# Second biases of a graph layer and a mixture of experts: from a product in the output sums to rows loaded under the experts' results

## The chip, the cores and the metric

The kernel runs on one core of one Trainium2 chip. The core has five engines that each work through their own instructions in order: TensorE (PE: matrix products and transposes, with its weight loads shown apart as PEld), VectorE (DVE), ScalarE (ACT), GpSimd (POOL) and SyncE (SP). They wait for each other by semaphores. SP, ACT and POOL also issue transfers (DMAs), which 16 DMA engines carry out. The metric is the time of one execution on the device in microseconds (us); lower is better.

## The reference, cut to what matters

625 rows of 1024 numbers pass through a graph convolution over 20,000 edges and then through a mixture of experts. The change concerns the second part alone, for x normalised:

```python
sh = _gelu(jnp.einsum('td,sdh->sth', xf, sW1) + sb1[:, None, :])
shared = jnp.einsum('sth,shd->std', sh, sW2) + sb2[:, None, :]
shared = shared.mean(axis=0)
gates = xf @ rW + rb
topk_vals, topk_idx = jax.lax.top_k(gates, TOP_K)
topk_probs = jax.nn.softmax(topk_vals, axis=-1)
...
h = _gelu(jnp.einsum('td,edh->eth', xf, W1) + b1[:, None, :])
y = jnp.einsum('eth,ehd->etd', h, W2) + b2[:, None, :]
moe = jnp.einsum('te,etd->td', w, y)
return (shared + moe).reshape(B, L, D)
```

There are two shared experts and eight others, of which each row uses two (TOP_K), with weights that sum to one. The second biases are sb2 (2 x 1024) and b2 (8 x 1024).

## The kernel before

The kernel computes only what each row needs. One program holds the whole: a sparse path, and a dense one that runs only when the sparse path's tables overflow. The recording layer orders the instructions of each engine; `tc.issue_after` pins some of them, and the names below are those of the profile.

*The start.* SP loads the edges, x (xh), the graph weights (wg). POOL makes constants and issues small loads: rb_t (five), vec (two), bd (two), rw_t. Then VectorE makes one-hot matrices of the edges (ohs at L873 and L874, ohk at L877) and statistics of the rows (st at L776), and TensorE counts edges with them (cnt) and projects the rows (p_pr, L920). After the graph layer, normalised rows (h2) and sums (x1d) are written to DRAM.

*Routing.* `gate`, `route` and `slots` choose two experts per row and give each choice a place (slot) in one of NJ = 11 tiles of 128 rows. Seven tiles belong to one expert each (4 to 10), three (0 to 2) to two with 64 rows each, one (3) to four with 32 rows each. `ej` holds the expert numbers, read into registers (`e_of`), and `row` the row of the table `yt` in DRAM to which each slot's result goes. `wab` holds the two weights of each row.

*Experts.* For each tile POOL gathers its rows (`fetch`, into io tiles, three buffers), TensorE transposes and multiplies them (`expert_in`, p_h; `expert_mid`, p_hT). Then, in the order ORDER = 4, 5, 6, 0, 1, 2, 3, 7, 8, 9, 10, it multiplies by the second weights (p_yj, L1455; two halves of 512 columns, each in one of five banks of the tag acc). The halves are copied out (L1459 on VectorE, L1461 on ACT) to a tile ys, which POOL scatters to rows of yt (L1463). ys tiles, the copies w2m of second weights and the rows g read back from yt share the 15 buffers of the pool gat.

*Output.* SP loads the shared experts' second weights (sw2, L1434) and the sums x1 (five tiles of 125 rows, L1437) when the buffers of the first weights come free, and after the last scatter the rows g (L1474). TensorE makes the shared experts' sums p_o (eight products per block, L1510), VectorE adds half of it and the two weighted rows g to x1 (L1486), and SP and ACT store the rows.

*The biases.* `bias_parts` brings sb2 and b2 from the DRAM tile bd into the bfloat16 tile b23, split into three parts for accuracy; `weights_T` does the same with the rows' weights (1 for the shared ones, twice the softmax weight for the others) and has TensorE transpose them (p_wT, L1336) into wT. One more product per block, wT by b23 (L1512), puts all biases into p_o:

```python
            with tc.issue_after(made.ins):
                for i in range(NS):
                    for k in range(HK):
                        nc.tensor.matmul(p[:TP, :n], shT[:, i, k, own], sw2[:, i, k, at],
                                         start=(i == 0 and k == 0), stop=False)
                nc.tensor.matmul(p[:TP, :n], wT[:, own], b23[:, at], start=False, stop=True)
            add(x1[:, d, at], p[:TP, :n], 1.0 / NS, x1[:, d, at])
```

Of the kernel before, what the change touches and what calls it, by code (L numbers as in the profile page):

```python
# [18 lines left out]
N = 625  # L19
# [434 lines left out]
def sparse_kernel(  # L454
# [171 lines left out]
    for i in (2, 3):  # L626
        nc.gpsimd.tensor_add(join, join, ident[:, QC * i : QC * (i + 1)])


    bd = dram.tile([3, NS + NE, D], F32, name="bd")  # L630
    nc.gpsimd.dma_start(bd[:, :NS, :], bass.AP(tensor=sb2.tensor, offset=sb2.offset,
                                               ap=[[0, 3], [D, NS], [1, D]]))
    nc.gpsimd.dma_start(bd[:, NS:, :], bass.AP(tensor=b2.tensor, offset=b2.offset,
                                               ap=[[0, 3], [D, NE], [1, D]]))
    b23 = const.tile([3 * QC, D], BF16, name="b23")

    def bias_parts():
        b2x = io.tile([3 * QC, D], F32, tag="io", name="b2x")
        nc.vector.memset(b2x, 0.0)
        for j in range(3):  # L640
            nc.gpsimd.dma_start(b2x[j * QC : j * QC + 3 * (NS + NE)], bd.rearrange("i e d -> (i e) d"))
        b2h = rt.tile([3 * QC, D], BF16, name="b2h")
        for j in range(3):
            with tc.issue_after(named.ins):
                nc.vector.tensor_copy(b2h, b2x)
            nc.scalar.copy(b23[j * QC : (j + 1) * QC], b2h[j * QC : (j + 1) * QC])
            if j < 2:
                nc.vector.tensor_sub(b2x, b2x, b2h)

    rw_t = const.tile([128, KD, QC], F32, name="rw_t")  # L650
    nc.vector.memset(rw_t[:, :, NE:], 0.0)
# [369 lines left out]
    def clear():  # L1021
        nc.gpsimd.memset(zero, 0.0)
        for a in range(2):
            to = bass.AP(tensor=yt.tensor, offset=yt.offset + (a * YB + 1) * D,
                         ap=[[NT * D, 128], [D // 2, 2 * NT], [1, D // 2]])
            nc.sync.dma_start(to, zero[:, None, :].to_broadcast([128, 2 * NT, D // 2]))

    at(50, clear)
    at(100, last_rows)
    at(30, transpose_vec)  # L1030
# [101 lines left out]
        nc.vector.tensor_copy(gates, pv[:, :, :NE])  # L1132


    w = const.tile([TP, NT, NS + NE], F32, name="w")
    wT = hid.tile([3 * QC, N], BF16, name="wT")
    sel = const.tile([TP, NT, NE], F16, name="sel")
    wide = [TP, NT, NE]

    def route():  # L1140
        full = [TP, NT, NE, NE]
        other = gates[:, :, None, :].to_broadcast(full)
        own = gates[:, :, :, None].to_broadcast(full)
        nc.vector.tensor_scalar(lower, lower, 0.0, None, op0=ALU.is_gt)
        above = rt.tile(full, F32, name="above")
        equal = rt.tile(full, F32, name="equal")
        nc.vector.tensor_tensor(above, other, own, op=ALU.is_gt)
        nc.vector.tensor_tensor(equal, other, own, op=ALU.is_equal)
# [15 lines left out]
        nc.vector.memset(w[:, :, :NS], 1.0)  # L1164
        nc.vector.tensor_mul(w[:, :, NS:], ex, inv[:, :, None].to_broadcast(wide))


    shT = hid.tile([128, NS, HK, N], F32, name="shT")
# [19 lines left out]
    def slots():  # L1188
# [66 lines left out]
        nc.vector.tensor_mul(m, m, w[:, None, :, NS:].to_broadcast(both_))  # L1255
# [61 lines left out]
        nc.vector.tensor_tensor(flag, flagf[:, 0:1], flagf[:, 1:2], op=ALU.add)  # L1317
        return named

    def weights_T():  # L1320
        nc.vector.tensor_scalar(w[:, :, NS:], w[:, :, NS:], float(NS), None, op0=ALU.mult)
        NW_ = NS + NE
        part = rt.tile([TP, NT, 3 * QC], F32, name="part")
        nc.vector.memset(part, 0.0)
        near = const.tile([TP, NT, NW_], BF16, name="near")
        for i in range(3):
            nc.vector.tensor_copy(near, w)
            for j in range(3):
                at = j * QC + i * NW_
                nc.vector.tensor_copy(part[:, :, at : at + NW_], near)  # L1330
            if i < 2:
                nc.vector.tensor_sub(w, w, near)
        for a, b in ((0, 3), (3, NT)):
            p = ps_mm(f"p_wT_{a}")
            for d in range(a, b):
                nc.tensor.transpose(p[: 3 * QC, (d - a) * TP : (d - a + 1) * TP], part[:, d, :],  # L1336
                                    ident[:TP, :TP])
            nc.vector.tensor_copy(wT[:, a * TP : b * TP], p[: 3 * QC, : (b - a) * TP])

    gate()  # L1340
    route()
    named = slots()
    weights_T()
    bias_parts()
    for t in range(HK):
        shared_in(1, t)
    sh_in.close()
# [4 lines left out]
    xts = ExitStack()  # L1352
    xt = pool(xts, "xt", 2, side="right")
    _, e_of = nc.values_load_multi_w_load_instructions(
        ej, engines=[mybir.EngineType.PE, mybir.EngineType.Activation], min_val=0, max_val=NE - 1,
        skip_runtime_bounds_check_because="a count of eight ends at most, cut to seven")


# [69 lines left out]
    xts.close()  # L1428
    in_w.close()

    late = pool(ctx, "late", side="right")
    sw2 = late.tile([128, NS, HK, D], F32, name="sw2")
    for i in range(NS):
        nc.sync.dma_start(sw2[:, i], sW2[i].rearrange("(k p) d -> p k d", p=128))  # L1434
    x1 = late.tile([TP, NT, D], F32, name="x1")
    for t in range(NT):
        nc.sync.dma_start(x1[:, t, :], x1d[t * TP : (t + 1) * TP, :])  # L1437
    gat = pool(ctx, "gat", 15, side="right")

    ORDER = (*whole[:3], *range(NM2), *whole[3:])  # L1440
    w2m = {}
    for j in ORDER:
        for a, _, e in parts(j)[1:]:
            for k in range(HK):
                w2m[j, a, k] = gat.tile([128, D], F32, tag="y", name=f"w2m_{j}_{a}_{k}")
                nc.scalar.copy(w2m[j, a, k][:, None, :], w2a[:, bass.ds(e, 1), k, :])
    sent = []
    for n, j in enumerate(ORDER):
        y = gat.tile([128, D], F32, tag="y", name=f"ys_{j}")
        for s in range(2):  # L1450
            at = slice(s * 512, (s + 1) * 512)
            p = ps_acc(f"p_yj_{j}_{s}")
            for k in range(HK):
                for a, b, e in parts(j):
                    made = nc.tensor.matmul(p[a:b], hjT[:, j, k, a:b],  # L1455
                                     w2m[j, a, k][:, at] if a else w2a[:, bass.ds(e, 1), k, at],
                                     start=(k == 0), stop=(k == HK - 1))
# [12 lines left out]
    for d in range(NT):  # L1470
# [26 lines left out]
    for d in range(NT):  # L1497
        if d == LATE:
            for i in range(d, NT):
                add_experts(i)  # L1500
        own = slice(d * TP, (d + 1) * TP)
        for at in ((0, 512), (512, D)) if d < NT - 1 else ((0, 512), (512, 768), (768, D)):
            n = at[1] - at[0]
            at = slice(*at)
            p = (ps_mm if banks % 8 > 4 else ps_acc)(f"p_o_{d}_{at.start}")
            banks += 1
            with tc.issue_after(made.ins):
                for i in range(NS):
                    for k in range(HK):
                        nc.tensor.matmul(p[:TP, :n], shT[:, i, k, own], sw2[:, i, k, at],  # L1510
                                         start=(i == 0 and k == 0), stop=False)
                nc.tensor.matmul(p[:TP, :n], wT[:, own], b23[:, at], start=False, stop=True)  # L1512
# [48 lines left out]
```

## Time and profile before

| | us |
|---|---|
| median of 3 runs | 295.12 |
| lowest and highest | 292.23, 295.93 |
| the profiled execution | 294.8 |
| its span, first to last instruction | 293.0 |
| PE busy | 283.4 (97%) |
| DVE busy | 168.3 (57%) |
| ACT busy | 103.2 (35%) |
| POOL busy | 44.1 (15%) |

The profile is of one execution, so durations and positions are compared with its own 294.8 us. Busy time is that of an engine's instructions; a wait counts to none. A chain of waits is followed back from the last instruction: at each step to what released it, or to the instruction before it on its engine. "Granted clock" is TensorE's clock as a share of full speed; DMA share is the mean busy share of the 16 DMA engines.

### The profile page before, as it was taken

To read this page: it belongs to the slowest core of one execution; us is meant where nothing else is said; L and a number is where in the kernel's file an instruction comes from. 1 tells how busy PE (TensorE), PEld (TensorE's weight loads), DVE (VectorE), ACT (ScalarE), POOL (GpSimd) and SP (SyncE) were. 2 spreads that over 40 slices of the span, in tenths; PEclk is the share of its full clock that TensorE was granted. 3 is DMA by queue.
4 is the path that set the end of the run, shared out by engine and by line. 5 is a ranking of instruction groups with operands and counts; after the bars stand their busy time and mean duration, and the time that the engine had idled before them with its cause. 6 is when DMAs were issued, how large, how long until landed. Compare 5 with 4: busy or idle time off the path is not lost.

```text
span 293.0 us, 4532 instructions
## 1 busy us (share of the span) xinstructions
PE 283.4 (97%) x1573; PEld 192.1 (66%) x1573; DVE 168.3 (57%) x459; ACT 103.2 (35%) x237; POOL 44.1 (15%) x101
## 2 busy tenths in 40 slices
PE   7998999999999999899999999999999999999992
PEld 5876777778888555677777987778643334444451
DVE  5699999997874888746925322222134111157920
ACT  2348425513642323353105544656198111000000
POOL 9500000000000024420131312110012223200000
PEclk9999999999999999999999999999999999999998
DMA  6999930000000999999999742420095545389351
GB/s 229 344 322 408 408 117 2 2 1 2 0 0 4 327 364 392 393 392 369 409 353 408 283 143 78 140 74 0 2 342 230 211 194 226 136 332 403 134 156 53
DMA packets 28699, 61.41 MB, mean 210 GB/s; under 512 B 2150, under 2 KB 15981, under 8 KB 28666
## 3 DMA queue, kind: packets, MB, share of 16 engines
q1 hardware_dynamic: 23144, 44.17, 42.0%
q0 software_dynamic: 5232, 16.55, 15.4%
q10 hardware_dynamic: 296, 0.35, 0.5%
q8 instruction: 15, 0.25, 0.3%
q14 instruction: 12, 0.10, 0.1%
HBM read 43.02 MB, written 18.81 MB: 211 GB/s over the span
## 4 chain that ended last, share of the span: by engine, by line
PE 77%; DVE 20%; issue 1%; ACT 1%; ACTq 0%; DVEq 0%
PE p_h L1397 13%; PE p_yj L1455 13%; PE p_o L1510 12%; PE p_sh L1175 11%; PE p_pr L920 9%; PE p_agg L937 5%; PE p_x L1378 3%; DVE ohs L873 3%; DVE ohs L874 2%; PE p_y L983 2%; PE scrap L1000 2%; DVE xh L987 2%; DVE st L776 2%; DVE xh L807 1%; DVE ohk L877 1%; DVE h L747 1%
## 5 line engine op out<-in xcount | busy, mean ns | idle before, releaser
L920 PE MATMUL p_pr<-wg,nT 128*125 128x286 f32 x240 | 61.5, 409 | 1.0 <-ACT nT L825 0.8
L920 PEld LDWEIGHTS p_pr<-wg,nT 128*125 128x125 f32 x240 | 43.8, 187 | 13.2 <-ACT nT L825 1.8
L1397 PE MATMUL p_h<-w1a,xsT 128*128 (+2 forms) x176 | 40.0, 381 | 0.0
L1455 PE MATMUL p_yj<-w2a,hjT 128*128 (+2 forms) x88 | 38.6, 595 | 0.0
L1510 PE MATMUL p_o<-sw,shT 128*125 128x512 f32 (+1 forms) x88 | 36.1, 554 | 0.0
L1175 PE MATMUL p_sh<-h2T,sw 128*128 128x313 f32 (+1 forms) x128 | 35.2, 429 | 0.0
L1397 PEld LDWEIGHTS p_h<-w1a,xsT 128*128 128x128 f32 (+2 forms) x176 | 28.8, 169 | 7.4 <-issue 0.5
L1175 PEld LDWEIGHTS p_sh<-h2T,sw 128*128 128x128 f32 x128 | 23.7, 190 | 8.6 <-issue 0.2
L1455 PEld LDWEIGHTS p_yj<-w2a,hjT 128*128 128x128 f32 (+2 forms) x88 | 14.4, 169 | 22.4 <-issue 22.4
L1510 PEld LDWEIGHTS p_o<-sw,shT 128*125 128x125 f32 x88 | 16.4, 188 | 16.9 <-issue 16.2
L1459 DVE COPY ys<-p_yj 128x512 f32<-128x512 f32 x15 | 10.4, 692 | 28.7 <-PE p_yj L1455 27.0
L1401 DVE COPY hj<-p_h 128x256 f32<-128x256 f32 x11 | 4.7, 425 | 31.1 <-PE p_h L1397 31.1
L994 POOL DMA_DIRECT2D x1d<-xh x10 | 5.3, 531 | 92.4 <-DVE flagf L721 89.0
L983 PE MATMUL p_y<-wo_t,eT 128*125 128x512 f32 (+1 forms) x40 | 18.8, 592 | 0.0
L1463 POOL DMA_INDIRECT yt<-ys,row x11 | 10.8, 981 | 50.5 <-DVE ys L1459 50.5
L1412 ACT ACTIVATE hjT<-p_hT,vT 128x128 f32<-128x128 f32 (+2 forms) x34 | 8.7, 332 | 24.5 <-PE p_hT L1409 24.5
L1486 DVE SCALAR_TENSOR_TENSOR x<-p_o,x 125x512 f32<-125x512 f32 (+1 forms) x11 | 6.9, 639 | 16.3 <-PE p_o L1512 16.3
L1370 POOL DMA_INDIRECT xs<-h2d,tok x11 | 10.4, 948 | 34.5 <-PE p_x L1378 24.9
L937 PE MATMUL p_agg<-P,CT 125*125 125x288 f32 x100 | 15.5, 305 | 0.0
L1397 PE MATMUL p_h<-w1m,xsT 128*64 128x256 f32 (+1 forms) x96 | 14.7, 382 | 0.0
L1455 PE MATMUL p_yj<-w2m,hjT 128*64 128x512 f32 (+1 forms) x48 | 14.1, 595 | 0.0
L1382 DVE COPY xsT<-p_x 128x512 f32<-128x512 f32 x11 | 7.6, 692 | 11.0 <-PE p_x L1378 8.7
(309 smaller groups left out, 422.8 us busy)
## 6 DMA issues: line engine op xcount, KB each, us to landing
w1a<-in_L_ffn_W_dram SPq DMA_DIRECT2D x8, 1024.0 KB
w2a<-in_L_ffn_W_dram SPq DMA_DIRECT2D x8, 1024.0 KB
yt<-zero SPq DMA_DIRECT2D x2, 2560.0 KB
g<-yt SPq DMA_DIRECT2D x10, 512.0 KB
sw<-in_L_ffn_sW_dram SPq DMA_DIRECT2D x4, 1024.0 KB
x<-x1d SPq DMA_DIRECT2D x5, 500.0 KB
x1d<-xh POOLq DMA_DIRECT2D x5, 448.0 KB, 7.2
h2d<-h POOLq DMA_DIRECT2D x5, 448.0 KB, 6.8
```

The source lines that it names most:

```text
L873: nc.vector.tensor_tensor(os, row[:, None].to_broadcast(shape), key, op=ALU.is_equal)
L920: nc.tensor.matmul(p[:TP, :F], nT[:, k, m * TP : (m + 1) * TP], wg[:, k, r, :], start=(k == 0), stop=(k == KD - 1))
L937: nc.tensor.matmul(p[:TP, : F + 2], CT[:, m, at : at + TP], P[:, m, r, i], start=(m == 0 and i == 0), stop=(m == NT - 1 and i == 1))
L983: nc.tensor.matmul(ps[s][:TP, :], eT[:n, k, :], wo_t[:n, k, at], start=(k == 0), stop=False)
L1175: nc.tensor.matmul(p[:, : z - a], sw1[:, i, k, t * 128 : (t + 1) * 128], h2T[:, k, a:z], start=(k == 0), stop=(k == KD - 1))
L1370: nc.gpsimd.indirect_dma_start(out=xs, out_offset=None, in_=h2d, in_offset=bass.IndirectOffsetOnAxis(ap=tok[:, j : j + 1], axis=0))
L1378: nc.tensor.transpose(p[:, k * 128 : (k + 1) * 128], xs[:, at : at + 128], ident)
L1397: nc.tensor.matmul(p[a:b, :H], xsT[j][:, k, a:b], w1m[j, a][:, 0, k, :] if a else w1a[:, bass.ds(e, 1), k, :], start=(k == 0), stop=(k == ...
L1455: made = nc.tensor.matmul(p[a:b], hjT[:, j, k, a:b], w2m[j, a, k][:, at] if a else w2a[:, bass.ds(e, 1), k, at], start=(k == 0), stop=(k = ...
L1459: nc.vector.tensor_copy(y[:, at], p)
L1463: sent.append(nc.gpsimd.indirect_dma_start(out=yt, out_offset=bass.IndirectOffsetOnAxis(ap=row[:, j : j + 1], axis=0), in_=y, in_offset=No ...
L1510: nc.tensor.matmul(p[:TP, :n], shT[:, i, k, own], sw2[:, i, k, at], start=(i == 0 and k == 0), stop=False)
```

## The change

The biases leave the output sums. At the start the kernel loads sb2 and b2 into a tile bt; `bias_table` makes b2 plus the mean of sb2 of it, one row for each of the eight experts, and writes it to bd in DRAM. As the two weights of a row sum to one, a row of that table under each of its two results gives the same sum. SP loads the table's row of each tile's expert, chosen by a register, into all of its ys tile's partitions (one transfer for a tile of one expert, two or four for the others) before the products are there, and VectorE adds each half product to it. The first three tiles of ORDER use io buffers, the others gat; the last five are asked for as the loop goes on. `weights_T`, `bias_parts`, wT, b23 and the product L1512 go.

```diff
-    bd = dram.tile([3, NS + NE, D], F32, name="bd")
...
+    BF = D * NE // 128
+    bd = dram.tile([NE, D], F32, name="bd")
+    bt = fbig.tile([128, NS + 1, BF], F32, name="bt")
+    for i in range(NS):
+        nc.gpsimd.dma_start(bt[:, i, :], bass.AP(tensor=sb2.tensor, offset=sb2.offset + i * D,
+                                                 ap=[[0, NE], [BF, D // BF], [1, BF]]))
+    nc.gpsimd.dma_start(bt[:, NS, :], b2.rearrange("e (q f) -> (e q) f", f=BF))
+
+    def bias_table():
+        nc.vector.tensor_add(bt[:, 0, :], bt[:, 0, :], bt[:, 1, :])
+        nc.vector.scalar_tensor_tensor(bt[:, NS, :], bt[:, 0, :], 1.0 / NS, bt[:, NS, :],
+                                       op0=ALU.mult, op1=ALU.add)
+        nc.gpsimd.dma_start(bd.rearrange("e (q f) -> (e q) f", f=BF), bt[:, NS, :])
...
+    at(46, bias_table)
     at(50, clear)
...
-    weights_T()
-    bias_parts()
...
-        ej, engines=[mybir.EngineType.PE, mybir.EngineType.Activation], min_val=0, max_val=NE - 1,
+        ej, engines=[mybir.EngineType.PE, mybir.EngineType.Activation, mybir.EngineType.SP], min_val=0, max_val=NE - 1,
...
+    ORDER = (*whole[:3], *range(NM2), *whole[3:])
+    ys, put = {}, {}
+
+    def bias_rows(j, y):
+        for a, b, e in parts(j):
+            put[j] = nc.sync.dma_start(y[a:b, :], bd[bass.ds(e, 1), :].to_broadcast([b - a, D]))
+        ys[j] = y
+
+    for j in ORDER[:3]:
+        bias_rows(j, io.tile([128, D], F32, tag="io", name=f"ys_{j}"))
...
+    for j in ORDER[3:6]:
+        bias_rows(j, gat.tile([128, D], F32, tag="y", name=f"ys_{j}"))
+    sw2 = late.tile([128, NS, HK, D], F32, name="sw2")
+    for i in range(NS):
+        with tc.issue_after(put[ORDER[5]].ins):
+            nc.sync.dma_start(sw2[:, i], sW2[i].rearrange("(k p) d -> p k d", p=128))
+    x1 = late.tile([TP, NT, D], F32, name="x1")
+    for t in range(NT):
+        with tc.issue_after(put[ORDER[5]].ins):
+            nc.sync.dma_start(x1[:, t, :], x1d[t * TP : (t + 1) * TP, :])
     sent = []
     for n, j in enumerate(ORDER):
-        y = gat.tile([128, D], F32, tag="y", name=f"ys_{j}")
+        y = ys[j]
...
-            if s or n < 4:
-                nc.vector.tensor_copy(y[:, at], p)
-            else:
-                nc.scalar.copy(y[:, at], p)
+            nc.vector.tensor_add(y[:, at], y[:, at], p)
...
+        if n + 6 < NJ:
+            bias_rows(ORDER[n + 6], gat.tile([128, D], F32, tag="y", name=f"ys_{ORDER[n + 6]}"))
...
-                nc.tensor.matmul(p[:TP, :n], wT[:, own], b23[:, at], start=False, stop=True)
```

More of the change, by code (lines that the diff above doesn't have):

```diff
@@ L627, in sparse_kernel @@
         nc.gpsimd.tensor_add(join, join, ident[:, QC * i : QC * (i + 1)])
-    bd = dram.tile([3, NS + NE, D], F32, name="bd")
[L631 to L648, printed above, removed]
+    BF = D * NE // 128
[10 more added lines that the diff above has]
+        nc.gpsimd.dma_start(bd.rearrange("e (q f) -> (e q) f", f=BF), bt[:, NS, :])
     rw_t = const.tile([128, KD, QC], F32, name="rw_t")
@@ L1132, in gate @@
         nc.vector.tensor_copy(gates, pv[:, :, :NE])
-    w = const.tile([TP, NT, NS + NE], F32, name="w")
-    wT = hid.tile([3 * QC, N], BF16, name="wT")
+    w = const.tile([TP, NT, NE], F32, name="w")
     sel = const.tile([TP, NT, NE], F16, name="sel")
@@ L1163, in route @@
         nc.vector.reciprocal(inv, tot)
-        nc.vector.memset(w[:, :, :NS], 1.0)
-        nc.vector.tensor_mul(w[:, :, NS:], ex, inv[:, :, None].to_broadcast(wide))
+        nc.vector.tensor_mul(w, ex, inv[:, :, None].to_broadcast(wide))
     shT = hid.tile([128, NS, HK, N], F32, name="shT")
@@ L1254, in slots @@
         nc.vector.tensor_tensor(m, m, ab[:, :, :, None].to_broadcast(both_), op=ALU.is_equal)
-        nc.vector.tensor_mul(m, m, w[:, None, :, NS:].to_broadcast(both_))
+        nc.vector.tensor_mul(m, m, w[:, None, :, :].to_broadcast(both_))
         nc.vector.tensor_reduce(wab, m, axis=AX.X, op=ALU.add)
@@ L1318, in slots @@
         return named
[L1320 to L1338, printed above, removed]
     gate()
@@ L1429, in sparse_kernel @@
     in_w.close()
-    late = pool(ctx, "late", side="right")
[L1432 to L1437, printed above, removed]
+    ORDER = (*whole[:3], *range(NM2), *whole[3:])
[6 more added lines that the diff above has]
+        bias_rows(j, io.tile([128, D], F32, tag="io", name=f"ys_{j}"))
+    late = pool(ctx, "late", side="right")
     gat = pool(ctx, "gat", 15, side="right")
-    ORDER = (*whole[:3], *range(NM2), *whole[3:])
     w2m = {}
@@ L1510, in sparse_kernel @@
                         nc.tensor.matmul(p[:TP, :n], shT[:, i, k, own], sw2[:, i, k, at],
-                                         start=(i == 0 and k == 0), stop=False)
-                nc.tensor.matmul(p[:TP, :n], wT[:, own], b23[:, at], start=False, stop=True)
+                                         start=(i == 0 and k == 0), stop=(i == NS - 1 and k == HK - 1))
             add(x1[:, d, at], p[:TP, :n], 1.0 / NS, x1[:, d, at])
```

## The prediction

> **What bounds the kernel now.** I read the page first: TensorE is busy 97% of the span. Then busy time by stage, cut where the chain of waits changes character (columns: stretch and length, then busy us of PE, PEld, DVE, ACT, POOL, granted TensorE clock, DMA share, GB/s):
>
> ```profile
> 11.80:52.00 40.20, 39.00 (x261) 30.24 (x259) 39.97 (x119) 19.22 (x54) 0.96 (x10) 1.00 0.71 249
> 123.90:213.20 89.30, 89.30 (x621) 69.21 (x622) 33.53 (x134) 37.50 (x78) 14.01 (x18) 1.00 0.62 221
> 213.20:250.60 37.40, 37.40 (x136) 14.53 (x135) 9.69 (x14) 17.08 (x27) 9.82 (x10) 1.00 0.60 239
> 250.60:287.20 36.60, 36.56 (x99) 17.59 (x98) 19.55 (x22) 0.00 (x0) 0.98 (x1) 1.00 0.63 232
> 287.20:293.00 5.80, 0.00 (x0) 0.00 (x0) 0.42 (x1) 0.00 (x0) 0.00 (x0) 0.87 0.11 31
> ```
>
> From 123.9 us on TensorE never stops: there, only TensorE's own work and new waits of TensorE count. From 11.8 to 52 us VectorE is full as well (39.97 of 40.20), and TensorE nearly so (39.00): a hole made there in either is not made up.
>
> The chain of waits, early, in the middle and late (start, us, what):
>
> ```profile
> 12.45 0.34 DVE ohs L873
> 12.80 0.02 issue
> 12.82 0.42 DVE ohs L874
> ```
>
> ```profile
> 147.45 0.54 PE p_wT L1336 x5
> ```
>
> ```profile
> 213.20 37.40 PE p_yj L1455 x134
> 250.60 3.43 PE p_o L1510 x8
> 254.03 0.22 PE p_o L1512
> ```
>
> The first shows the set end on VectorE's instructions back to back; the others what the bias path takes of TensorE.
>
> Then the queues that the change uses. POOL's early loads in the timeline, and the DMA issues of that stretch with KB each and us from issue to landing:
>
> ```profile
> 7.60 0.85 POOL L631 DMA_DIRECT2D bd<-in_L_ffn_sb_dram  x1
> 9.88 0.55 POOL L633 DMA_DIRECT2D bd<-in_L_ffn_b_dram  x1 [1.15 <-DMA rb_t<-in_L_ffn_rb_dram]
> ```
>
> ```profile
> bd<-in_L_ffn_b_dram POOLq DMA_DIRECT2D x1, 96.0 KB, 7.1
> rw_t<-in_L_ffn_rW_dram POOLq DMA_DIRECT2D x1, 32.0 KB, 7.4
> vec<-in_L_ffn_sb_dram POOLq DMA_DIRECT2D x1, 2.0 KB, 5.5
> ```
>
> SP's late issues in the timeline, and what SP's queue (q1) and POOL's (q0) moved from 211 to 219, from 219 to 248 and from 248 to 255 us (packets, MB, share of 16 engines):
>
> ```profile
> 211.81 1.50 SPq L1434 DMA_DIRECT2D sw<-in_L_ffn_sW_dram  x2
> 213.36 11.38 SPq L1437 DMA_DIRECT2D x<-x1d  x5
> ```
>
> ```profile
> q1 hardware_dynamic: 540, 2.09, 69.9%
> ```
>
> ```profile
> q0 software_dynamic: 1201, 3.87, 33.5%
> q1 hardware_dynamic: 646, 2.55, 22.2%
> ```
>
> ```profile
> q1 hardware_dynamic: 8, 0.02, 0.7%
> ```
>
> The 2.09 MB are the two sw2 loads (2 x 1024 KB), done by 219. The 2.55 MB are the five x1 loads (5 x 500 KB): 29 us at 0.088 MB/us, on 22.2% of 16, or 3.6 engines. They are slow and end at about 248, and nobody minds: VectorE's first add into x1 is at 254.3.
>
> **The change part by part.** The sum is made against the profiled execution, 294.8 us (span 293.0 and 1.8 around it); the median of the three runs, 295.12, is 0.3 above, inside their spread of 3.7.
>
> Removed from TensorE where it never stops: nine L1512 products of 0.22 us and the last two of 0.11 and 0.13, together 2.22; the five p_wT transposes, 0.54. **-2.76 us.** Leaving weights_T and bias_parts also frees VectorE (five 1024-wide passes alone are 3 x 0.69 + 2 x 1.22 = 4.5 us), ACT (3 x 1.04) and POOL (1.49 of b2x loads, so the first gathers leave earlier): nothing, since TensorE had 89.30 us of work in 89.30 throughout.
>
> Evictions: 22 adds on VectorE instead of 15 copies there and 7 on ACT. The nearest row, the add of a product to SBUF data of the same shape (L987), took 0.68 us, the copy 0.69. 22 x 0.68 = 15.0 us in a stretch of 37.4 on an engine with nothing else there: nothing, hidden by TensorE. If the adds have to wait, this cover goes; see below.
>
> The table, early. In the instruction order of the changed program bias_table does not stand at count 46: its first add is VectorE's instruction right behind the first one-hot comparison (ends 12.78), before L874 of the chain above. It waits for both sb2 loads. The first goes out where L631 did (7.60), the second where L633 did, at 9.88, as it waits for the same rb_t landing. Landing of POOL's small loads around it: 4.9 (rb_t, median), 5.2 and 5.5 (vec), 5.7, 7.1, 7.4 us. The load (32 KB in 128 pieces) falls between the last two in time; I take 6.3, between the vec rows and those two: 9.88 + 6.3 = 16.2, a stall of 3.4, and 0.2 for two 64-wide instructions. Behind it wait the one-hots, the second tile's statistics and thus transposes and projection: TensorE, out of its first projection at 15.5, waits as well, and neither has room to catch up. **+3.6 us**, bounds 2.1 (4.8 us) to 4.7 (7.4). The b2 load follows at 10.7 and lands at 17.0; VectorE needs it 2 us after the stall, at 18: nothing. The write of the table stands in POOL's queue before stores first due at 101.9, after 89 us of idleness: nothing.
> [...]
>
> The table, late. SP now reads the expert numbers too, behind the flag that it read at 145 us: nothing. Its queue becomes: ORDER[0..2] (tiles 4, 5, 6; io buffers, free by 204.5, landed well before 214), then six pieces for ORDER[3..5] from 211.8, then sw2, then x1, and only then ORDER[6..10]: tile 3 in four pieces, 7, 8, 9, 10. The three tiles ahead are 1.5 MB; at the 0.37 MB/us that sw2 had (213.3 to 219) they move sw2's end from 219 to 223.1. It is due at 250.4: nothing. But x1's start moves too. From 223.1 to about 242 (last scatter before the hold-up lands) at 0.088 MB/us or a little better, 1.7 MB; the rest, 0.85 MB, with no scatter beside it, at 0.124 (0.088 over 3.55 engines is 0.0248 an engine; 3.55 busy, with the scatters' 33.5% taken off each, are 3.55 / 0.665 = five engines in use): x1 ends at about 249. Tile 3's rows are queued behind it on those engines: 249 + 1.3 (32 KB an engine) + 1.2 until the landing is signalled (bounds 0 and 3.2, the shortest whole landing of a POOL transfer) = 251.5.
> Who waits: the add of ORDER[6], whose product TensorE has at 235.0. Behind it on VectorE wait all later adds; behind those the scatters, and TensorE once five acc banks are full. Halves run 1.72 us: five before the end of p_yj, TensorE needs that bank back, at 250.6 - 5 x 1.72 = 242.0. So it stands from 242.0 to 251.5 + 0.8 = 252.3: **+10.3 us.** Bounds: x1 at 0.124 throughout (ends 243.7) 3.8; at 0.088 throughout (252.1) and 3.2 until signalled 15.4. The remaining rows then follow one each 1.3 us or so, faster than TensorE asks. The tail (last scatter, reads of yt, adds) moves with it.
>
> After the stand TensorE's clock. In the last 5.8 us without a product the granted clock averages 0.87: how deep it falls no row tells. I assume one half: then it fell 4.3 us after the last product, and if it takes as long to return, 4.3 us at half speed lose **2.1 us**. Bounds 0 and twice that, 4.3; the middle, since no restart is in this trace.
> [...]
>
> Sum: 294.8 - 2.76 + 3.6 + 10.3 + 2.1 = **308.0 us**. Lowest: 294.8 - 2.76 + 2.1 + 3.8 = 297.9; highest: 294.8 - 2.76 + 4.7 + 15.4 + 4.3 = 316.4.
>
> **The rivals.**
> Not slower: tile 3's rows land by 241.2, because transfers behind x1 pass it. For it: x1 uses few engines, the others are free. Against: every piece spreads over partitions on all of them, so its last part waits. Then 294.8 - 2.76 + 3.6 = 295.6. It decides at 241.2, the 242.0 less 0.8.
> Faster or equal: besides that the early load lands before 12.8, in 2.9 us. The shortest landing of any POOL transfer was 3.2 (a scatter). 292.0 or, with the two instructions, 292.2.
> Slower still: 128 reads of one 4 KB row are slow. No row reads one row so often. At x1's 0.088 MB/us a tile of 0.5 MB takes 6 us; the last five, from 249 on, end at 279, and TensorE ends p_yj some 30 us late: 325. It decides above about 3.4 us a tile, TensorE's own pace.
>
> **How the numbers follow.** Hold-up behind x1: 0.80. No hold-up, early stall only: 0.10. All hidden: 0.04. Slow reads: 0.06. About 2% (5.9 us) is what a measurement of this kernel can tell from no change: below 289.2 faster, above 301.0 slower. Slower: 0.76 of the first (its low corner is under 301.0) and 0.06, 0.82; faster 0.01; the rest, 0.17, within. The range is the bounds of the first case, 298 to 316; the other three, 0.20, lie outside.
>
> **What would show it.** The changed profile should have L1512's and L1336's rows gone; VectorE idle for 3 to 4 us near 13 us "<-DMA bt"; one idle stretch of TensorE of some 10 us in p_yj, before the half that reuses the bank of ORDER[6]; VectorE's add of that tile waiting for "ys<-bd", SP's queue at 20 to 30% until then; a granted clock under 1.00 behind it. No idle TensorE there means x1 does not hold the rows. Adds that wait tile after tile mean slow reads.

## The result, and the profile after

The changed kernel takes 317.89 us (median of 4 runs, 317.35 to 318.51) where the kernel before takes 294.68 beside it (292.23 to 295.93): 1.080 times as long, 95% interval 1.072 to 1.088. The profiled execution took 318.29 us, its span 316.4, so 23.4 us more span than before. 308.0 was predicted, with 316 as the upper end: the direction and both places were right, the size was not.

Line numbers move: L1512 and L1336 are gone, p_yj is L1440, its adds L1443, row loads L1407, sw2 L1427, x1 L1431, p_o L1494, the table's first add L639.

VectorE's timeline of the changed kernel around the table (start, us, what, and in brackets the idle time before it and what ended it):

```profile
12.24 0.42 DVE L867 TENSOR_TENSOR ohs<-iota,cols 125x512 f16<-125x512 f16 x1
16.52 0.23 DVE L639 TENSOR_TENSOR bt<-bt 128x64 f32<-128x64 f32 x1 [3.86 <-DMA bt<-in_L_ffn_sb_dram]
16.66 0.42 DVE L868 TENSOR_TENSOR ohs<-ohs,cols 125x512 f16<-125x512 f16 x1
```

The second one-hot instruction stood at 12.82 before and stands at 16.66 now: 3.84 us. TensorE behind it, before and after, in each kernel's timeline of that engine:

```profile
15.76 1.07 PE L819 MATMUL p_t<-ident,h 125*128 125x125 f32 x8
16.87 4.12 PE L920 MATMUL p_pr<-wg,nT 128*125 128x286 f32 x16
```

```profile
19.60 1.93 PE L813 MATMUL p_t<-ident,h 125*128 125x125 f32 x8 [2.00 <-ACT h L780]
21.32 5.80 PE L914 MATMUL p_pr<-wg,nT 128*125 128x286 f32 x16
```

The transposes start 3.84 later too, but they and the projection also take longer. Busy time in stretches of 3 us shows why (columns as before: stretch and length, busy us of PE, PEld, DVE, ACT, POOL, granted clock, DMA share, GB/s):

```profile
14.00:17.00 3.00, 1.48 (x7) 0.81 (x5) 0.48 (x3) 0.00 (x0) 0.00 (x0) 1.00 1.06 259
17.00:20.00 3.00, 0.68 (x6) 0.66 (x7) 2.93 (x10) 0.81 (x2) 0.72 (x1) 0.68 1.10 301
20.00:23.00 3.00, 3.00 (x12) 2.55 (x11) 2.31 (x9) 1.13 (x4) 0.00 (x0) 0.50 1.10 380
23.00:26.00 3.00, 3.00 (x10) 2.15 (x10) 3.00 (x15) 1.33 (x2) 0.00 (x0) 0.68 1.02 390
```

The granted clock falls to 0.50 here already; nothing in the prediction had that. Now the late stand, in the list of waits (who, for whom: us, times, longest) and the chain of waits:

```profile
PE p_yj L1440 <- DVE ys L1443: 17.8, 1, 17.8
DVE ys L1443 <- DMA ys<-bd: 25.2, 1, 25.2
```

```profile
247.02 17.38 DMA ys<-bd
...
264.52 0.70 DVE ys L1443
...
265.27 11.52 PE p_yj L1440 x20
276.78 34.37 PE p_o L1494 x88
```

One stand of TensorE, 17.8 us long, ended by VectorE's add of tile 3, which waits for that tile's row: as foretold, but for 10.3. The stages of TensorE around it, cut at the last hj copy, the stand and the restart:

```profile
217.30:246.90 29.60, 29.60 (x120) 11.19 (x119) 8.65 (x13) 13.48 (x22) 5.92 (x6) 1.00 0.74 263
246.90:265.20 18.30, 0.58 (x2) 0.00 (x0) 0.68 (x2) 0.00 (x0) 0.00 (x0) 0.59 0.62 188
265.20:276.80 11.60, 11.53 (x21) 5.09 (x22) 5.30 (x9) 0.00 (x0) 3.90 (x4) 0.76 0.48 192
276.80:311.20 34.40, 34.34 (x88) 16.10 (x87) 19.57 (x22) 0.00 (x0) 0.97 (x1) 1.00 0.66 240
```

p_o's stage is 34.40 where it was 36.60: the products are gone, at their full price. The five halves of the restart take 11.52 where five take 8.6: 2.9 more, at a clock of 0.76. SP's issues tell where the row was:

```profile
221.90 1.10 SPq L1427 DMA_DIRECT2D sw<-in_L_ffn_sW_dram  x2
223.04 17.57 SPq L1431 DMA_DIRECT2D x<-x1d  x5
240.88 22.62 SPq L1407 DMA_DIRECT2D ys<-bd  x8
```

and what the queues moved from 219 to 222, from 228 to 231 and from 237 to 240 us (packets, MB, share of 16 engines; q1 is SP's, q0 POOL's scatters):

```profile
q1 hardware_dynamic: 205, 0.69, 78.5%
```

```profile
q1 hardware_dynamic: 177, 0.66, 54.2%
q0 software_dynamic: 158, 0.59, 48.4%
```

```profile
q1 hardware_dynamic: 68, 0.27, 21.7%
q0 software_dynamic: 140, 0.40, 33.7%
```

First the row pieces of ORDER[3..5], 0.23 MB/us; then sw2, 0.22 beside scatters; then x1, at the 0.09 it had before. The bytes of rows and sw2 (1.57 and 2.10 MB) are through at 234.2: x1 starts there. The prediction had it at 223.1, 228.5 with the shift of 5.4 that the early loss measured at the last hj copy (211.85, now 217.29).

The span's 23.4 us by stage: up to the last hj copy +5.44 (0.54 of transposes saved, 3.84 of wait; the remaining 2.14 I put down to the clock: half speed from TensorE's restart at 19.60 to 24.9 costs up to 2.65), stand +17.8, restart +2.9, p_o -2.2, tail -0.55 (5.25 for 5.80).

### The profile page after: what moved, and what is told of

The parts are those of the page before. It is cut to its first block, busy times and chain, and to the rows that moved or that the text cites. A ratio compares the mean times of both kernels' runs of the same rounds, so it can differ in the third digit from the quotient of the medians.

```text
span 316.4 us, 4534 instructions
## 1 busy us (share of the span) xinstructions
PE 286.2 (90%) x1557; PEld 192.6 (61%) x1557; DVE 165.0 (52%) x443; ACT 95.8 (30%) x227; POOL 43.8 (14%) x100
## 4 chain that ended last, share of the span: by engine, by line
PE 67%; DVE 10%; DMA 9%; SPq 9%; issue 2%; ACT 1%; POOL 1%; DVEq 0%; POOLq 0%; ACTq 0%
PE p_pr L914 16%; PE p_h L1368 12%; PE p_o L1494 11%; PE p_sh L1168 10%; SPq L1431 5%; DMA ys<-bd 5%; PE p_agg L931 4%; PE p_yj L1440 4%; PE p_x L1349 3%; SPq L1407 3%; DMA bt<-in_L_ffn_sb_dram 2%; DMA rb_t<-in_L_ffn_rb_dram 2%; PE p_y L977 2%; DVE xh L981 2%; PE cnt L893 2%
## 5 line engine op out<-in xcount | busy, mean ns | idle before, releaser
L914 PE MATMUL p_pr<-wg,nT 128*125 128x286 f32 x240 | 63.6, 418 | 0.7 <-ACT nT L819 0.6
L1440 PE MATMUL p_yj<-w2a,hjT 128*128 (+2 forms) x88 | 41.5, 629 | 17.8 <-DVE ys L1443 17.8
L914 PEld LDWEIGHTS p_pr<-wg,nT 128*125 128x125 f32 x240 | 44.6, 192 | 13.2 <-ACT nT L819 1.3
L1440 PEld LDWEIGHTS p_yj<-w2a,hjT 128*128 128x128 f32 (+2 forms) x88 | 15.3, 180 | 42.2 <-issue 23.1
L1443 DVE TENSOR_TENSOR ys<-ys,p_yj 128x512 f32<-128x512 f32 x22 | 14.9, 686 | 44.9 <-DMA ys<-bd 25.2
L1494 PE MATMUL p_o<-sw,shT 128*125 128x512 f32 (+1 forms) x88 | 34.5, 553 | 0.0
L1494 PEld LDWEIGHTS p_o<-sw,shT 128*125 128x125 f32 x88 | 16.5, 187 | 18.3 <-issue 17.9
L931 PE MATMUL p_agg<-P,CT 125*125 125x288 f32 x100 | 15.5, 305 | 0.0
L813 PE MATMUL p_t<-ident,h 125*128 125x125 f32 x80 | 11.8, 300 | 3.0 <-ACT h L780 2.0
```

What stands on the lines that cost most here:

```text
L813: nc.tensor.transpose(pv[:, k, :], row[:, at : at + 128], ident[:TP, :TP])
L914: nc.tensor.matmul(p[:TP, :F], nT[:, k, m * TP : (m + 1) * TP], wg[:, k, r, :], start=(k == 0), stop=(k == KD - 1))
L931: nc.tensor.matmul(p[:TP, : F + 2], CT[:, m, at : at + TP], P[:, m, r, i], start=(m == 0 and i == 0), stop=(m == NT - 1 and i == 1))
L1440: made = nc.tensor.matmul(p[a:b], hjT[:, j, k, a:b], w2m[j, a, k][:, at] if a else w2a[:, bass.ds(e, 1), k, at], start=(k == 0), stop=(k = ...
L1443: nc.vector.tensor_add(y[:, at], y[:, at], p)
```

## The experiments

Theory A: x1's five 125-row loads, on few DMA engines (21.7% of the 16 above), hold tile 3's row. Theory B: the table's first add stalls VectorE early, and TensorE's clock falls behind that (0.50 above). Rivals: the DMA engines are short of bandwidth as a whole; rows read over and over are slow; the queue's order alone does it.

**x1 in 112 and 13 rows.**

```diff
-        with tc.issue_after(put[ORDER[5]].ins):
-            nc.sync.dma_start(x1[:, t, :], x1d[t * TP : (t + 1) * TP, :])
+        for g in PARTS:
+            with tc.issue_after(put[ORDER[5]].ins):
+                nc.sync.dma_start(x1[g, t, :], x1d[t * TP + g.start : t * TP + g.stop, :])
```

> Each of x1's five 125-row loads becomes two, of 112 and 13 rows; the queue and its order stay. Theory A (x1 holds the rows behind it because a 125-row load runs on few engines): the 2.5 MB then run at the 0.25 MB/us that sw2 had beside scatters in the changed kernel, 10 us from 234 instead of 28; the row of tile 3 lands at about 246, TensorE wants its bank back at about 247: TensorE's stand shrinks from 17.8 us to 0 to 2, and the time is 297 to 301. Rival 1 (the transfers as a whole are short of bandwidth, scatters and rows and x1 together): x1 still ends near 260, stand above 12 us, time above 312. Rival 2 (the rows of the table themselves are slow to read): the adds wait one after another, time above 312.

301.3 us, ratio 1.019 (1.011 to 1.026). 16.6 us less than the changed kernel, for the same bytes in the same order. From 237 to 240 the queue moves 0.71 MB where it moved 0.27, with about the same scatters. A stand is left (the page's group; the profile is of the slowest of its four executions):

```profile
L1441 PE MATMUL p_yj<-w2a,hjT 128*128 (+2 forms) x88 | 41.5, 628 | 4.4 <-DVE ys L1444 4.4
```

4.4 us where I expected 0 to 2. Presumably sw2 and x1 ahead of the row cost something as bytes too; no run separates that.

**x1 from ACT's queue.** The 125 rows are kept.

```diff
-            nc.sync.dma_start(x1[:, t, :], x1d[t * TP : (t + 1) * TP, :])
+            nc.scalar.dma_start(x1[:, t, :], x1d[t * TP : (t + 1) * TP, :])
```

> x1's five loads keep their 125 rows and are issued from ACT's queue instead of SP's. If it is the order in SP's queue that holds the rows, tile 3's row comes right behind sw2, by 240, and TensorE does not stand: 295 to 299, with x1 itself still slow. If the few engines that x1 uses are the hold-up whatever the queue, the pieces of the rows on those engines still wait: a stand above 10 us, 310 or more. If each engine divides itself between the two queues, rows land a few us later than alone, and the time is below 302.

317.05 us: nothing is won. What the queues moved from 231 to 234 us (q10 is ACT's), and a line of SP's own list of waits:

```profile
q0 software_dynamic: 110, 0.39, 32.4%
q10 hardware_dynamic: 56, 0.21, 17.0%
q1 hardware_dynamic: 1, 0.00, 0.0%
```

```profile
SPq L1407 <- DMA x<-x1d: 23.4, 3, 9.8
```

SP's queue stands still although nothing of x1 is in it, but not because engines hold its loads: after 224.05 SP issued nothing until 234.01, and by the list each of these issues was released by the landing of a tile of x1. Whether the program or the transfers make SP wait so is not shown. The row pieces issued at 223.58 and 234.01 had landed by 229.7 and 242.4, while x1 went on until 259.8. So another queue does not free the rows, but this run cannot tell the engines from the order of issue; the runs with x1 in parts and with its place changed have to.

**Table late, first attempt; and with x1 in parts.** The add was held behind an instruction of ACT; the second kernel also has x1 in 112 and 13 rows, as above.

```diff
-        nc.vector.tensor_add(bt[:, 0, :], bt[:, 0, :], bt[:, 1, :])
+        with tc.issue_after(outs[-1].ins):
+            nc.vector.tensor_add(bt[:, 0, :], bt[:, 0, :], bt[:, 1, :])
...
-    at(46, bias_table)
+    at(100, bias_table)
```

> The two instructions that make the table are held until most window counts are out; the rest is the changed kernel. Theory B (stall of VectorE at the first add, then a lower TensorE clock): the 6.0 us lost early are gone, the late stand stays at 17 to 18 us: 311.5 to 313. If the slower clock early has another cause than this stall, only 3.7 us go: about 314. If the late stand depends on absolute times of SP's queue alone and not on TensorE's progress, it grows by what is won early: 318.

> Table late and x1 in 112 and 13 rows, both. Theories A and B together: neither stand is left, only the 2.76 us of products and transposes taken from TensorE remain, 291.9, and up to 2 us of late wait: 291.5 to 294. If the removal is worth nothing, 294.7 or more; if one of the two stands has a cause that neither edit touches, above 300.

315.5 and 300.94. Both expectations fail for a dull reason: VectorE's order did not change. The add still waits, 4.5 and 3.1 us, right behind the first one-hot instruction. The runs count as repeats of the changed kernel and of x1 in parts, within 2.4 and 0.4 us.

**Table late, behind a VectorE instruction.** `counted` holds VectorE's instruction of each window count.

```diff
     def bias_table():
-        nc.vector.tensor_add(bt[:, 0, :], bt[:, 0, :], bt[:, 1, :])
+        with tc.issue_after(counted[-1].ins):
+            nc.vector.tensor_add(bt[:, 0, :], bt[:, 0, :], bt[:, 1, :])
...
-    at(46, bias_table)
+    at(100, bias_table)
```

> The first instruction of the table is held behind the last window count's VectorE instruction so far, so that it stands some hundred instructions further down in VectorE's order; the rest is the changed kernel. Theory B (the early loss is VectorE's stall at this add and the TensorE clock behind it): the shift of 5.4 us at the end of the expert stage goes, VectorE has no wait for the table, no fall of the clock before 60 us; the late stand stays at 17 to 18 us: 311 to 313. Rival (the hold-up late is set by the DMA engines' own clock of work and takes back what is won early): 316 or more.

311.58 us (311.23 to 312.71), ratio 1.059 (1.052 to 1.066): 6.3 less than the changed kernel, all of the early loss; the late stand stays, 18.3 us:

```profile
11.69 0.41 DVE L868 TENSOR_TENSOR ohs<-iota,cols 125x512 f16<-125x512 f16 x1
12.14 0.43 DVE L869 TENSOR_TENSOR ohs<-ohs,cols 125x512 f16<-125x512 f16 x1
```

The two one-hot instructions follow each other as before the change. From 8 to 30 us the granted clock is 1.00. B holds; the rival that the late stand would take it back falls.

**x1 behind the rows, table late.** One tile of x1, in two parts, goes out behind each of the five later row loads.

```diff
-    for t in range(NT):
-        with tc.issue_after(put[ORDER[5]].ins):
-            nc.sync.dma_start(x1[:, t, :], x1d[t * TP : (t + 1) * TP, :])
...
             bias_rows(ORDER[n + 6], gat.tile([128, D], F32, tag="y", name=f"ys_{ORDER[n + 6]}"))
+            for g in PARTS:
+                with tc.issue_after(put[ORDER[n + 6]].ins):
+                    nc.sync.dma_start(x1[g, n, :], x1d[n * TP + g.start : n * TP + g.stop, :])
```

> Table late, and x1's loads in 112 and 13 rows, one tile of x1 behind each of the five later row loads in SP's queue instead of all ahead of them. Theory A (rows wait behind x1): tile 3's row is issued when its buffer comes free, about four tiles into the output products, behind sw2 alone, and lands some 5 us before its product is due; each later row with its x1 tile (1 MB) needs 4.3 us at 0.235 MB/us against 3.4 us of TensorE per tile, with 7 us of slack: no stand, 291.5 to 294. Rival 1 (the DMA engines as a whole have too little for rows, sw2, x1 and scatters): a stand of 3 us or more remains, 297 or more.

291.75 us (289.73 to 292.25), ratio 0.989 (0.982 to 0.997): 1.1% under the kernel before, clear of 1 but inside the 2% that the prediction took as the measure of a change. In its chain of waits TensorE runs through, as long in p_yj as before the change:

```profile
212.51 37.40 PE p_yj L1438 x134
249.91 34.37 PE p_o L1495 x88
```

Bandwidth as a whole is enough. The late hold-up costs 311.58 - 291.75 = 19.8 us.

**No x1.**

```diff
-    for t in range(NT):
-        with tc.issue_after(put[ORDER[5]].ins):
-            nc.sync.dma_start(x1[:, t, :], x1d[t * TP : (t + 1) * TP, :])
+    nc.vector.memset(x1, 0.0)
```

> The changed kernel with x1's loads left out: x1 starts as zeros written by VectorE, so the output lacks the residual. Theory A (x1 is what holds the rows): the first row behind sw2 lands by about 238 and TensorE does not stand; the early stall stays: 318 less 17.8 and 2.9, 296 to 299. If rows are late without x1 as well (same-row reads, scatters, sw2 ahead), a stand above 3 us and a time above 301.

295.58 us, just under the forecast, and no stand in p_yj. Without x1 the row is in time. The 3.8 us left over 291.75 I put down to the early stall, which is in its profile (VectorE waits 5.6 us for the table's load); it costs less here than in the other runs.

**Other rows in place of one.** On the kernel with x1 behind the rows:

```diff
-            put[j] = nc.sync.dma_start(y[a:b, :], bd[bass.ds(e, 1), :].to_broadcast([b - a, D]))
+            put[j] = nc.sync.dma_start(y[a:b, :], h2d[bass.ds(e, b - a), :])
```

> As the kernel with x1 interleaved and the table late, but each row load reads as many different rows of another tensor (the normalized rows, from the same register) instead of one row over and over: the biases are replaced by other numbers. In the changed kernel the queue moved 0.23 MB/us at 95% busy while it read rows of the table, where sw2 had 0.36 at 90%. If reading one row over and over is what is slow, the queue moves 0.35 or more per us while ORDER[3..5] load, and that stretch is 2 us shorter; the time falls only by what stand the interleaved kernel has left, 0 to 2 us. If different rows are as slow, the rate stays at 0.23 and the cause is the shape of the load or the writing side.

291.39 us, and from 213 to 216 us the queue moves as little as with one row (0.74 MB there):

```profile
q1 hardware_dynamic: 218, 0.73, 95.0%
```

Reading one row over and over is not slower than reading different rows; that rival falls.

**Before, without the bias path.**

```diff
-    weights_T()
-    bias_parts()
...
-                                         start=(i == 0 and k == 0), stop=False)
-                nc.tensor.matmul(p[:TP, :n], wT[:, own], b23[:, at], start=False, stop=True)
+                                         start=(i == 0 and k == 0), stop=(i == NS - 1 and k == HK - 1))
```

> The kernel before with the whole second-bias path left out (products L1512, weights_T, bias_parts and their loads), so the output lacks the second biases. The prediction's first step: 2.22 of products and 0.54 of transposes leave a TensorE that never stops, 291.4 to 292.4 beside a before of about 294.7. Rival (the engine's time is not the end's time): no change.

291.93 us against 294.89, ratio 0.990 (0.987 to 0.993): 2.96 less, close to the 2.76 worked out. The interleaved kernel has all of this, with its biases.

**Interleaved, x1 in 125 rows.**

```diff
-            for g in PARTS:
-                with tc.issue_after(put[ORDER[n + 6]].ins):
-                    nc.sync.dma_start(x1[g, n, :], x1d[n * TP + g.start : n * TP + g.stop, :])
+            with tc.issue_after(put[ORDER[n + 6]].ins):
+                nc.sync.dma_start(x1[:, n, :], x1d[n * TP : (n + 1) * TP, :])
```

> As the kernel with x1 interleaved and the table late, but each x1 tile is one load of 125 rows again. If the order in the queue is enough, no stand, 291 to 293. If a 125-row load holds the pieces of the next row on the few engines it uses, as the run with x1 on ACT's queue says, each later row comes some 6 us behind the one before (500 KB on five engines beside scatters) against TensorE's 3.4 a tile: tile 10 lands near 254, about 5 us after its product, two or three stalls of 1 to 4 us: 293 to 299.

297.67 us, ratio 1.010 (1.006 to 1.014). VectorE's last four pairs of adds:

```profile
241.01 1.28 DVE L1441 TENSOR_TENSOR ys<-ys,p_yj 128x512 f32<-128x512 f32 x2 [4.65 <-PE p_yj L1438]
247.84 1.29 DVE L1441 TENSOR_TENSOR ys<-ys,p_yj 128x512 f32<-128x512 f32 x2 [5.54 <-PE p_yj L1438]
254.41 1.28 DVE L1441 TENSOR_TENSOR ys<-ys,p_yj 128x512 f32<-128x512 f32 x2 [5.29 <-DMA ys<-bd]
261.04 1.28 DVE L1441 TENSOR_TENSOR ys<-ys,p_yj 128x512 f32<-128x512 f32 x2 [5.35 <-DMA ys<-bd]
```

A row every 6.6 us, not every 3.4; the last two adds wait for the row itself. With an x1 tile ahead of each row that is the pace of the x1 tiles. Shape and order are both needed. What ends this kernel is the last scatter and the reads behind it (VectorE waits 7.7 us for g), not TensorE, which hardly stands.

**The early loss alone, and TensorE kept busy through it.** Interleaved, with the table at its early place; then with 34 and with 90 spare products behind the first projection.

```diff
     project(0)
+    scrap = ps_acc("scrap2")
+    warm(34)
     count_windows(between)
```

> x1 interleaved as in the fastest run so far, but the table left at its early place: the early loss alone. VectorE waits 2.5 to 5 us for the table's load, by when the load lands; where TensorE's clock falls as well the loss is about 6, where it does not 2 to 3: 294.5 to 298.5. Rival (the clock and the wait have nothing to do with the table): 291.75.

> The same, with 34 products of 128 columns into a bank of their own put on TensorE right behind its first projection, 3.8 us of work at the rate of the 22 ahead of it (2.46 us), so that TensorE does not idle while VectorE waits. If the fall of the clock is what makes the early loss larger than the wait, the second projection's 16 products take 4.1 us again and the time falls by 2 to 2.5 us against the same kernel without them; if the clock falls for another reason, no change or up to 1 us slower.

> The kernel with x1 interleaved and the table early, with 90 products of 128 columns behind the first projection (the 34 took 2.06 us, so 5.4 us), which end behind the landing of the table's load. If idleness of TensorE is what lowers its clock, the granted clock stays at 1.00 until 60 us, the second projection's 16 products take 4.1 us where they took 4.6 to 5.8, and the time is 294.5 to 296, against 297.2 without them; the wait of VectorE, 2.5 to 6, stays. If the clock falls all the same, it does not come from idleness, and the time is 298 or more, as the 90 products come on top.

The early loss alone: 297.21 us, 5.5 above the interleaved kernel, and spread out (ten runs, 294.89 to 298.97). With 34 products 297.27, which tells nothing: they took 2.06 us, not 3.8, and in the profiled execution the load came late (VectorE waited 6.1), so TensorE idled all the same. With 90, 301.76: the time that I expected is missed by 6 us. The clock says more. First the kernel without spare products, then the one with 90:

```profile
14.00:17.00 3.00, 1.90 (x11) 1.18 (x9) 1.47 (x5) 0.00 (x0) 0.00 (x0) 1.00 1.06 258
17.00:20.00 3.00, 1.38 (x7) 1.38 (x8) 2.83 (x10) 1.05 (x3) 0.72 (x1) 0.68 1.09 311
```

```profile
17.00:20.00 3.00, 3.00 (x57) 3.00 (x55) 2.93 (x10) 0.70 (x2) 0.72 (x1) 1.00 1.09 294
20.00:23.00 3.00, 1.74 (x25) 1.47 (x21) 3.00 (x15) 0.11 (x1) 0.00 (x0) 1.00 1.10 371
23.00:26.00 3.00, 0.00 (x0) 0.00 (x0) 3.00 (x18) 1.98 (x4) 0.00 (x0) 0.74 1.04 403
```

With TensorE busy through the wait the clock stays at 1.00. It falls later, in a hole that the kernel did not have: the order on ACT has changed, the second tile's eviction nT now comes behind the normalisation of the third, and TensorE idles 5.4 us for it. So the clock fell in a hole of TensorE in both, and the spare products bought a worse order.

**Whole rows.** On the kernel with x1 behind the rows, each tile is filled by one load over 128 partitions.

```diff
-        for a, b, e in parts(j):
-            put[j] = nc.sync.dma_start(y[a:b, :], bd[bass.ds(e, 1), :].to_broadcast([b - a, D]))
+        e = parts(j)[0][2]
+        put[j] = nc.sync.dma_start(y, bd[bass.ds(e, 1), :].to_broadcast([128, D]))
```

> As the kernel with x1 interleaved and the table late, but the tiles made of two halves or four quarters get the row of their first expert by one load over 128 partitions instead of one load per piece: their other tokens get a wrong bias. In every run so far the queue moved 0.23 to 0.25 MB/us at over 90% busy while ORDER[3..5] loaded in pieces of 64 and 32 partitions. If the pieces are what is slow, that stretch goes at 0.35 or more, sw2 begins 2 us earlier, and the time stays at 291 to 292.5, since no stand is left to win. If the rate stays at 0.25, it is not the pieces.

292.21 us. From 213 to 216 us, rows and perhaps the head of sw2:

```profile
q1 hardware_dynamic: 251, 0.91, 87.0%
```

0.30 MB/us instead of 0.23 to 0.25, short of the 0.35 that I asked for, but on a smaller share: MB per engine-time is up by 26% (0.91 / 87.0 against 0.74 / 89.4). The pieces are a good part of the slowness; whether all of it stays open.

**No scatters.** On the kernel with the table late and x1 ahead of the rows:

```diff
-        sent.append(nc.gpsimd.indirect_dma_start(
-            out=yt, out_offset=bass.IndirectOffsetOnAxis(ap=row[:, j : j + 1], axis=0), in_=y, in_offset=None,
-            bounds_check=2 * YB - 1, oob_is_err=False))
-        for s in sent[:-1]:
-            tc.declare_no_dep(sent[-1].ins, s.ins, reason="rows of different slots")
```

> As the kernel with the table late alone, but the scatters into the per-token buffer are left out, so the output lacks the experts. The prediction's step (x1's 125 rows run at 0.088 MB/us because scatters take a third of its five engines, 0.124 without them): sw2 at 0.37 ends about 222, x1 at 0.124 ends about 243, tile 3's row lands at 245, a stand of 4 to 6 us, 297 to 300. If x1 is slow by itself, 0.07 to 0.09 with or without scatters, it ends at 251 or later, a stand of 11 us or more: 305 to 311.

304.56 us, a stand of 10.6: between the two forecasts. From 228 to 231, x1 alone in the engines:

```profile
q1 hardware_dynamic: 99, 0.39, 32.0%
```

0.13 MB/us on 32.0% of 16, 5.1 engines. Alone x1 does run as fast as the prediction's 0.124 said. Yet the row lands at 251.75 (in the chain of waits its last stretch begins at 234.27 and lasts 17.48), not at 245 as expected with x1 done at 243.

## Why the prediction was wrong in size, point by point

Three terms failed: the clock behind the early stall was put at nothing and cost 2.1 us; x1's start was worked out 5.7 us too early; and x1's pace behind the last scatter, put at 0.124 MB/us, was about 0.11, some 4.5 us more.

**Removed work, -2.76: right.** Left out by itself it is 2.96; in the changed kernel p_o is 2.2 shorter.

**Evictions at nothing: right.** The adds take 686 ns, and the interleaved kernel has all 22 of them with TensorE at full pace.

**The early stall, +3.6: the place and the wait were right, a term was missing.** The load landed in 6.85 us for 6.3, the stall is 3.84. The step let TensorE wait "as well" and resume at full speed. Its clock fell to 0.50 instead, and I put 2.14 us down to that: 6.0 in all, beyond the bound of 4.7. The sum had a clock term behind the late stand and none behind this one, though the text itself had TensorE wait there from 15.5 on. By the runs with the table moved the early loss is 5.5 to 6.3 us (3.8 without x1). Not every hole brought the fall: with x1 on ACT's queue TensorE's first projection ended at 15.27, the next transposes began at 17.86, 2.6 us later, and the clock stayed at 1.00 (from 14 to 29 us); in the run with the early loss alone, 15.63 and 18.62, 3.0 us, it fell; in the changed kernel, 15.48 and 19.60, 4.1 us, it fell as well. Four counting products lay in each of the three holes. In the changed kernel's trace, in stretches of 0.1 us, the four in which its clock changes between 15 and 274 us are (the mean places the change within the stretch):

```profile
18.00:18.10 0.10, 0.00 (x0) 0.00 (x0) 0.10 (x1) 0.00 (x0) 0.00 (x0) 0.91 0.92 297
24.90:25.00 0.10, 0.10 (x1) 0.07 (x1) 0.10 (x3) 0.10 (x1) 0.00 (x0) 0.96 1.53 533
250.10:250.20 0.10, 0.00 (x0) 0.00 (x0) 0.00 (x0) 0.00 (x0) 0.00 (x0) 0.94 1.04 246
270.60:270.70 0.10, 0.10 (x2) 0.10 (x1) 0.00 (x0) 0.00 (x0) 0.10 (x1) 0.66 0.01 0
```

The clock is halved for 6.8 us and for 20.5 us, with 225.3 at 1.00 between. In the run with the early loss alone it is halved for about 3.4 us, from 18.1 to 21.4, worked out from its means of 0.68 from 17 to 20 and 0.76 from 20 to 23. What sets how long the half speed lasts, and why 2.6 us of hole left the clock at 1.00 where 3.0 us did not, is not shown.

**The late hold-up, +10.3: the mechanism was right, two terms were mis-sized.** TensorE stopped at 247.5 (265.27 less 17.8), where 242.0, with the early shift 247.4, was worked out; x1 was the cause (no stand without it, and none with it behind the rows). But:

*x1's start.* "At the 0.37 MB/us that sw2 had" took rows and sw2 at sw2's rate of before. Rows in pieces of 64 and 32 partitions go at 0.23, and sw2, pushed back into the scatters, at 0.22: x1 starts at 234.2 for 228.5, 5.7 late. Whole rows went 26% better per engine-time (0.91 MB at 87.0% for 0.74 at 89.4%); why is not shown (pieces of several tiles were under way together).

*x1's pace with rows beside it.* "With no scatter beside it, at 0.124" left out that rows would be under way then. SP's last three issues in this stretch are rows, each released, by the lists of waits, by the landing of a tile of x1. SP's list from 200 to 270 us in the changed kernel:

```profile
SPq L1407 <- DMA x<-x1d: 13.9, 4, 5.1
```

| kernel | x1 starts | SP's last three row issues | tile 3's row landed |
|---|---|---|---|
| changed | 234.2 | 253.51, 258.32, 263.17 | 264.4 |
| table late | 227.9 | 246.78, 251.48, 256.07 | 258.3 |
| table late, no scatters | 225.7 | 241.07, 245.86, 250.58 | 251.75 |

A tile of x1, 0.51 MB, takes 4.6 to 4.9 us: 0.105 to 0.111 MB/us, with the scatters over or left out, where x1 alone had 0.13. The row follows the last tile of x1 by 1.2 to 2.2 us. That the later rows' parts on x1's engines lay ahead of tile 3's row is ruled out: from its landing at 264.4 to 270 SP's queue still moved 0.85 MB, more than the one row issued last (0.52). Why x1 is slower beside rows is not shown.

Together, as an estimate: x1's start 5.7 later; 1.4 less, because more of x1 then lies behind the last scatter (247.5), which by the prediction's two rates ends x1 at 258.7; 4.5 more, as it ended at 263.2; 1.3 less, as the row came 1.2 behind x1 and not 1.3 + 1.2 (no run shows the 1.2 for the signal by itself). That is 7.5 more stand than predicted, beyond the bound of 15.4, which still began x1 at 223.1.

**The clock after the stand, +2.1: 2.9.** From 252 to 270 us the granted clock is 0.50, the half that was assumed; the trace before had it too, 0.50 from 291.5 us to its end, though the prediction found no row for it. It fell 2.7 us after TensorE's last product, not 4.3, and came back 5.4 us after the restart, not as long after as it took to fall. The term is inside the bounds, and its closeness is in part luck.

**The rivals.** Not slower: tile 3's row did not pass x1 in its queue. Its last piece was issued by 246.84. SP's queue from 249 to 250.5 us, with rows on all 16 engines, and from 252 to 253.5, back at five engines' worth:

```profile
q1 hardware_dynamic: 102, 0.42, 102.7%
```

```profile
q1 hardware_dynamic: 50, 0.19, 31.4%
```

So the parts of rows on other engines went beside x1, and the row landed only 1.2 us behind x1's last tile: the prediction's "its last part waits". Slow reads: fell with the other rows. That the range, built on the first case's bounds, ended at 316 is the fault of its two steps: bounds were taken over the unknowns that I had named, and neither the early clock nor the rates of the rows ahead of x1 and of x1 beside rows was among them.

## What to carry to other kernels

x1's loads of 125 rows, at 22.2% of the engines before and 21.7% here, cost nothing until something urgent was issued behind them; then TensorE stood 17.8 us. So read a slow load's share of the engines while it runs, and count every byte that lies ahead of the urgent one, from all queues, against the load's rate, measured beside what else will run (0.13 MB/us alone, 0.11 beside rows, 0.09 beside scatters). A new transfer also pushes back what it is put ahead of, into other traffic (sw2 went at 0.22 MB/us beside scatters for 0.37 before), so a rate is taken from the stretch in which the transfer will then lie. And where a stall leaves TensorE idle, price its clock as well as the wait: here holes of 3.0 and 4.1 us brought half the clock for 3.4 and 6.8 us, one of 2.6 us brought none. The cure for the early stall was the order of issue, the same work placed where nobody waits; for the late one it was the order together with loads of 112 and 13 rows.

## What the runs showed of the hardware that was not expected

- 125-row loads alone (no scatters, 228 to 231 us) moved 0.39 MB in 3 us, 0.13 MB/us, at 32.0% of 16 engines, 5.1 engines' worth. Beside scatters, in 112 and 13 rows, the queue moved 0.71 MB in 3 us instead of 0.27.
- Row loads in pieces of 64 and 32 partitions moved 0.74 MB in 3 us at 89.4% of the engines; whole ones 0.91 at 87.0%.
- TensorE's granted clock was at 0.50 for 6.8 us in and behind the early hole (18.1 to 24.9 us in the changed kernel) and for 20.5 us in and behind the late one (250.2 to 270.7). It fell to 0.50 early although four counting products of 0.28 us in all lay in the middle of its idle time (17.3 us, in the hole between the first projection and 19.60).
- Spare products meant to hold the clock changed the order of another engine and cost 4.5 us (301.76 for 297.21).
